# One graph-transformer layer on one core: keys and values of five blocks read during the last product job, the loads among the last messages spread anew, and two blocks of attention numerators instead of three ahead of the block loop

## The chip, the cores and the metric

The kernel runs on one core of one Trainium2 chip. The metric is the device time of that core in microseconds (us); lower is better. Of the runs of a kernel the median counts. A profile is one further execution, recorded instruction by instruction. Engines are called by their short names: PE (TensorE) multiplies matrices, with its weight loads as PEld; DVE (VectorE) and ACT (ScalarE) work element by element; POOL (GpSimd) here mainly issues gathers and loads; SP only issues DMAs.

## The reference

One layer on a graph with 1250 nodes, 1024 features and 20000 edges of 8 types. A relational graph convolution, a gate, a linear attention over all nodes and a feed-forward network with operands rounded to FP4 are added up, all in float32:

```python
xn = layernorm(x)
u  = xn @ root + bias + sum_r mean_{edges of type r into node}(xn[src]) @ weight[r]
z  = concat([u, xn]) @ w_gate + b_gate
h  = tanh(u) * z + xn * (1 - z)
# attention: 8 heads of 16; q and k are expanded to (1, a, a_i * a_j / sqrt(2))
kv, ks = sum_n k[n] v[n]^T, sum_n k[n]
mix = ((q @ kv) / max(q . ks, 1e-5)) @ w_out
x1 = x + h + mix
out = x1 + fp4(silu(fp4(ln(x1)) @ fp4(wg).T) * (fp4(ln(x1)) @ fp4(wu).T)) @ fp4(wd).T
```

## The kernel before, in words

The rows are 10 blocks of 128 nodes (`NB`, `BR`; the last has 98). The program is written as one list of steps for a tile framework, which puts waits between engines by itself. Each engine works its own list strictly in order. `issue_after(x)` adds an order: what is written inside stands after instruction x.

**Product jobs.** `product` (L532) multiplies all rows with one 1024 x 512 half of a weight matrix, as three matmuls of reduced-precision parts, called limbs (high, low and a difference; L552, L553, L554). `limb` cuts the next job's weights on DVE and ACT (L509 to L512) while the last piece of the present job runs. A job has nine pieces (blocks 0 and 1 together, then one block each). Counted from 0, jobs 0 to 12 are the relations (5 first halves, 8 second halves), 13 is QKV (written to `qkv_d`), 14 and 15 the root weight, 16 and 17 the lower half of the gate weight. Results go to DRAM (`y_d`, `root_d`, `gx_d`).

**Messages.** The 20000 sorted edges are 157 tiles (`ST`). For each feature half, a message gathers 128 rows of `y_d` (POOL, L464), scales them (ACT `hi` L475, DVE rest L477), builds a 0/1 matrix (DVE `sel` L473), sums rows of the same target with two matmuls (PE L480, L481), copies the sum (ACT L482) and stores it in `seg_d` (ACT's queue, L483). A gather is issued two tiles (`LAG`) before its use; there are 4 gather buffers and 2 to 3 of the others. Messages of half 0 go between the pieces of the jobs 5 to 12, those of half 1 between the pieces of 13 to 17, up to tile `EARLY` = 140. The rest comes after the last product.

**After the last product** (the `late` part, L726 on): one load of queries, keys and values of all blocks (L732, L733, on SP's queue); `mix_sums` (L735), the sums over all nodes; `mix_pairs(b)` (L750), products of keys and values on DVE (`kk`, L759) summed by PE (L763); `open_rows`, `open_first`, `open_rest`, which add up targets that cross tiles and end with a copy `osum` on ACT and an indirect add into `seg_d` (L831). A list `rest` of 13 of these has the remaining messages between its entries; from its entry 3 on each entry also issues one load of the list `behind` on POOL's queue (x, root and gx rows of blocks 0 and 1, `loads`, L660; four parts of the upper gate weight `wg`, L865) and, at first, one FFN weight load. Then follow `nodes` (the indirect gathers of summed messages into `u`, L666), the transposes of FFN weights (`ffn_weight`, L857), `mix_num(b)` for `FIRST` = 3 blocks (L670; the attention numerators: PE, then about 9 us of DVE), `mix_transposed`, and `gate_first` (L717), the first half of block 0's gate (L715). The load of `wo` comes last (L901).

**Block loop** (L981 to L996). `block(i)` adds u's parts (L925 or L929), transposes u, multiplies by `wg` (L937) and the attention by `wo` (L940), makes x1 (L944) and its FP4-rounded normalisation x2 (L948 on, quantiser lines L142 to L155). Then come `mix_num` of a block two ahead, `hidden` of the block before (transposes of x2, L163; L962) and `finish` of the one before that (L978).

Of the kernel before, what the change touches and what calls it, by code (L numbers as in the profile page):

```python
# [20 lines left out]
KC = D // 128  # L21
# [5 lines left out]
H, DH = 8, 16  # L27
FIRST = 3
LAG = 2
EARLY = 140  # L30
FW = 5
# [9 lines left out]
def block_rows(b):  # L41
    return slice(b * BR, min((b + 1) * BR, N))
# [7 lines left out]
def gps_layer(ctx: ExitStack, tc: tile.TileContext, x, src, dst, et, w_rel, w_root, bias,  # L50
# [466 lines left out]
    with ExitStack() as main:  # L517
# [106 lines left out]

        tiles = messages(1, 0, EARLY)
        for i in range(5):
            product(n0 + R + i, share(tiles, i, 5))
    limbs.close()
# [30 lines left out]

    def loads(b, q):  # L660
        loaded[b] = [ld.tile([BR, D], F32, name=name)[:rows_of(b)] for name in ("xt", "rt", "gx", "u")]
        return [lambda o=o, a=a: q.dma_start(o, a[block_rows(b), :])
                for o, a in zip(loaded[b], (x, root_d, gx_d))]
# [61 lines left out]
    with ExitStack() as late:  # L725
        op = late.enter_context(tc.tile_pool(name="op", bufs=1))  # L726
        pb = late.enter_context(tc.tile_pool(name="pb", bufs=4))
        fw = late.enter_context(tc.tile_pool(name="fw", bufs=FW))
        V.memset(kv[:, :, 256:257], 1.0)

        full, rest_n = (NB - 1) * BR, N - (NB - 1) * BR
        nc.sync.dma_start(qkv[:, :NB - 1, :384], qkv_d[:full, :].rearrange("(b p) c -> p b c", p=BR))  # L732
        nc.sync.dma_start(qkv[:rest_n, NB - 1, :384], qkv_d[full:, :])  # L733

        def mix_sums():  # L735
            ps = mm_tile()
            for b in range(NB):
                T.matmul(ps[:, :257], kv[:rows_of(b), b, :128], kv[:rows_of(b), b, :], start=(b == 0), stop=(b == NB - 1))
            V.scalar_tensor_tensor(h3(rl[:, :128]), h3(ps[:, :128]), 0.5, m8(DH), op0=ALU.mult, op1=ALU.mult)
            V.tensor_tensor(h3(rl[:, 128:256]), h3(ps[:, 128:256]), m8(DH), ALU.mult)  # L740
            V.tensor_scalar(rl[:, 256:264], mask8, ps[:, 256:257], None, op0=ALU.mult)
            ps = mm_tile()
            for b in range(NB):
                T.matmul(ps[:1, :128], ones[:rows_of(b), :1], kv[:rows_of(b), b, 128:256], start=(b == 0), stop=(b == NB - 1))
            V.tensor_copy(crow[:, :128], ps[:1, :128])
            V.memset(crow[:, 128:], float(N))

        bd_ps = []

        def mix_pairs(b):  # L750
            if b == 0:
                bd_ps.append(mm_tile())
            ps, n = bd_ps[0], rows_of(b)
            kks = []
            for c in range(4):
                kk = pb.tile([BR, 2, DH, DH], F32, name="kk")[:n]
                ck = kv[:n, b, c * 32:c * 32 + 32].rearrange("p (h i) -> p h i", h=2)
                cv = kv[:n, b, 128 + c * 32:128 + c * 32 + 32].rearrange("p (h e) -> p h e", h=2)
                V.tensor_tensor(kk, ck[:, :, None, :].to_broadcast([n, 2, DH, DH]),  # L759
                                cv[:, :, :, None].to_broadcast([n, 2, DH, DH]), ALU.mult)  # L760
                kks.append(kk.rearrange("p h e i -> p (h e i)"))
            for c, kk in enumerate(kks):
                T.matmul(ps[32 * c:32 * c + 32], kv[:n, b, 32 * c:32 * c + 32], kk,  # L763
                         start=(b == 0), stop=(b == NB - 1))
# [57 lines left out]


        s1, s2 = {}, [op.tile([128, HD], F32, name=f"s2{nh}") for nh in range(2)]
        for nh in range(2):
            V.memset(s2[nh][:B2], 0.0)

        def open_add(nh, i, n, ps):
            osum = op.tile([128, HD], F32, name="osum", bufs=2)
            evac(osum[:n], ps[:n])  # L830
            return G.indirect_dma_start(  # L831
                out=seg_d[nh][:, :], out_offset=bass.IndirectOffsetOnAxis(ap=orow[:n, i:i + 1], axis=0),
                in_=osum[:n, :], in_offset=None, compute_op=ALU.add).ins
# [20 lines left out]
        def ffn_weight(q, src, r0, n, c0, wide, o, chunks, col):  # L854
# [8 lines left out]

        behind = loads(0, G)
        behind += [lambda k=k: G.dma_start(wg[:, k:k + 2, :], w_gate[k * 128:(k + 2) * 128, :].rearrange(  # L865
            "(k p) n -> p k n", p=128)) for k in range(0, KC, 2)]
        behind += loads(1, G)
        there = []
        rest = [mix_sums, open_rows, lambda: (open_first(0), open_rest_rows(0), open_rest(0), open_first(1))]
        rest += [lambda b=b: mix_pairs(b) for b in range(NB)]  # L870
        done = EARLY
        for i, p in enumerate(rest):
            p()
            while done < ST + LAG and (done - EARLY) * len(rest) < (i + 1) * (ST + LAG - EARLY):
                message(1, done)
                done += 1
            if i >= 3:
                with tc.issue_after(gathered_last[0]):
                    behind.pop(0)()
                if len(there) < FW:  # L880
                    there.append(ffn_weight(S, *weights[len(there)]))

# [8 lines left out]
        with tc.issue_after(gathered_last[0]):  # L891
            for b in range(2):
                nodes(b, 0)
            open_rest_rows(1)
        for p in steps[:SUMS]:
            p()
        open_rest(1)
        gate_first()
        for p in steps[SUMS:]:
            p()  # L900
        nc.sync.dma_start(wo, w_out)  # L901
    first_nums = last_num[0]
# [3 lines left out]

    wk = ctx.enter_context(tc.tile_pool(name="wk", bufs=1))
    def block(b):

        rows, n = block_rows(b), rows_of(b)  # L910
        if b not in loaded:
            for p in loads(b, nc.sync):
                p()
        xt, rt, gx, u = loaded[b]
        with tc.issue_after(gathered_last[0]):
            for nh in range(0 if b >= 2 else 1, 2):
                nodes(b, nh)
# [9 lines left out]
        else:  # L927
            with tc.issue_after(first_nums):
                V.tensor_tensor(u, rt, u, ALU.add)  # L929
# [13 lines left out]
        x1 = wk.tile([BR, D], F32, name="x1", bufs=3)[:n]  # L943
        V.tensor_tensor(x1, sx, gx, ALU.add)  # L944

# [7 lines left out]

    def hidden(x1, x2):

        n = x1.shape[0]
        xqT = wk.tile([128, KC, BR], F32, name="xqT")
        transpose_cols(xqT, x2, n, D_CHUNKS, 0)
        pg, pu = mm_tile(), mm_tile()
# [23 lines left out]
    for i in range(NB + 2):  # L983
        if i < NB:
            ahead[i] = block(i)
        if i == 0:
            sums.close()
            psum_pools(ctx, "right", more=2)
        if i and i + FIRST - 1 < NB:
            mix_num(i + FIRST - 1)  # L990
        if i and i + FIRST - 2 < NB:
            mix_transposed(i + FIRST - 2)
        if 0 <= i - 1 < NB:
            hidden_rows[i - 1] = hidden(*ahead.pop(i - 1))
        if i >= 2:
            finish(i - 2, *hidden_rows.pop(i - 2))  # L996


# [25 lines left out]
```

## Time and profile before

| | us |
|---|---|
| runs | 1996.54, 1984.03, 1994.1 |
| median | 1994.1 |
| profiled execution | 1983.85 |
| its span, first to last instruction | 1982.1 |
| PE busy | 1869.1 (94%) |
| DVE, ACT, POOL busy | 1308.5, 747.7, 617.0 |
| mean granted TensorE clock | 0.974 |

The profiled execution is 10 us below the median, so a sum made from its rows is compared with 1983.85 first. Product jobs fill the time up to 1484.4 us; the stretch with the remaining messages lasts to 1577.5 us (last L481), then come the open sums and first gates, and block 1's gate starts at 1621.8 us. Busy times count an engine's instructions without its waits; a wait is listed with the engine and line that ended it. PEclk is the clock that the throttle granted, and the DMA share is the mean busy share of the 16 DMA engines.

### The profile page before, as it was taken

To read this page: it belongs to the slowest core of one execution; us is meant where nothing else is said; L and a number is where in the kernel's file an instruction comes from. 1 tells how busy PE (TensorE), PEld (TensorE's weight loads), DVE (VectorE), ACT (ScalarE), POOL (GpSimd) and SP (SyncE) were. 2 spreads that over 40 slices of the span, in tenths; PEclk is the share of its full clock that TensorE was granted. 3 is DMA by queue.
4 is the path that set the end of the run, shared out by engine and by line. 5 is a ranking of instruction groups with operands and counts; after the bars stand their busy time and mean duration, and the time that the engine had idled before them with its cause. 6 is when DMAs were issued, how large, how long until landed. Compare 5 with 4: busy or idle time off the path is not lost. (4 is left out here: it accounts for less than half of the span.)

```text
span 1982.1 us, 24076 instructions
## 1 busy us (share of the span) xinstructions
PE 1869.1 (94%) x7828; PEld 1272.4 (64%) x7828; DVE 1308.5 (66%) x2934; ACT 747.7 (38%) x1299; POOL 617.0 (31%) x590
## 2 busy tenths in 40 slices
PE   7999999999999999999999989999997888999998
PEld 5465447777777777777777877667673244544544
DVE  7988936777644566456546666766655758777765
ACT  5111421221224455545554455555553342222211
POOL 1022477885013233333332233343344410000000
PEclk9999999999999999999999999899897898999999
DMA  6266334444336767777676688777688842122100
GB/s 217 75 162 143 86 80 107 128 126 124 118 118 212 230 222 222 229 226 231 214 232 219 213 259 256 239 254 240 219 258 260 307 126 67 64 75 72 35 22 30
DMA packets 157976, 332.76 MB, mean 168 GB/s; under 512 B 26978, under 2 KB 34598, under 8 KB 157850
## 3 DMA queue, kind: packets, MB, share of 16 engines
q0 software_dynamic: 39616, 112.32, 21.9%
q10 hardware_dynamic: 77258, 142.48, 19.4%
q1 hardware_dynamic: 40976, 76.42, 12.4%
q8 instruction: 62, 1.02, 0.2%
q14 instruction: 64, 0.52, 0.1%
HBM read 184.41 MB, written 146.53 MB: 167 GB/s over the span
## 5 line engine op out<-in xcount | busy, mean ns | idle before, releaser
L552 PE MATMUL ab<-wH,xH 128*128 128x512 f32 (+2 forms) x1440 | 568.4, 395 | 3.1 <-issue 1.7
L554 PE MATMUL ab<-wD,xD 128*128 128x512 f32 (+2 forms) x1440 | 561.5, 394 | 5.1 <-DVE wD L512 4.6
L553 PE MATMUL ab<-wL,xL 128*128 128x512 f32 (+2 forms) x1440 | 564.8, 393 | 0.0
L464 POOL DMA_INDIRECT msg<-y_d,key x314 | 329.5, 1049 | 662.6 <-PE sm L481 333.6
L477 DVE SCALAR_TENSOR_TENSOR msg<-msg,weight,hi 128x512 fp32r<-128x512 f32 x314 | 234.0, 748 | 143.0 <-ACT hi L475 84.5
L554 PEld LDWEIGHTS ab<-wD,xD 128*128 128x128 f32 (+1 forms) x1440 | 268.1, 187 | 76.1 <-DVE wD L512 11.8
L552 PEld LDWEIGHTS ab<-wH,xH 128*128 128x128 f32 (+1 forms) x1440 | 270.3, 188 | 65.8 <-issue 2.7
L553 PEld LDWEIGHTS ab<-wL,xL 128*128 128x128 f32 (+1 forms) x1440 | 269.5, 187 | 63.9 <-DVE wL L511 0.5
L482 ACT COPY seg<-sm 128x512 f32<-128x512 f32 x314 | 182.4, 585 | 199.1 <-PE sm L481 150.8
L475 ACT ACTIVATE hi<-msg,weight 128x512 fp32r<-128x512 f32 x314 | 221.6, 721 | 80.2 <-DMA msg<-y_d,key 27.4
L390 POOL DMA_INDIRECT sort_d<-pay,row x160 | 208.3, 1302 | 61.6 <-issue 48.5
L560 ACT ACTIVATE yt<-ab 128x512 f32<-128x512 f32 (+2 forms) x180 | 106.1, 593 | 316.4 <-PE ab L553 276.1
L408 PE MATMUL mm<-wt,xnT 128*128 128x512 f32 (+1 forms) x480 | 220.9, 603 | 0.0
L561 DVE SCALAR_TENSOR_TENSOR yt<-ab,yt 128x512 f32<-128x512 f32 (+2 forms) x180 | 121.5, 680 | 146.5 <-ACT yt L560 140.4
L480 PE MATMUL sm<-hi,sel 128*128 128x512 f32 x314 | 133.9, 430 | 30.4 <-ACT hi L475 24.1
L481 PE MATMUL sm<-msg,sel 128*128 128x512 f32 x314 | 137.0, 436 | 24.4 <-DVE msg L477 24.4
L473 DVE TENSOR_SCALAR sel<-iota_n,last_row 128x128 fp32r<-128x128 f32 x314 | 89.6, 287 | 99.0 <-PE sm L481 94.7
L408 PEld LDWEIGHTS mm<-wt,xnT 128*128 128x128 f32 (+1 forms) x480 | 85.5, 188 | 86.6 <-issue 86.1
L510 ACT CAST wH<-h 128x512 fp32r<-128x512 f32 x144 | 88.6, 621 | 129.6 <-DVE h L509 117.2
L937 PE MATMUL mm<-wg,uT 128*128 128x512 f32 (+1 forms) x288 | 126.4, 592 | 0.0
L511 DVE TENSOR_TENSOR wL<-raw,h 128x512 fp32r<-128x512 f32 x144 | 98.1, 681 | 26.5 <-PE mm L408 26.5
L962 PE MATMUL mm<-wguT,xqT 128*128 128x352 f32 (+1 forms) x320 | 101.2, 476 | 10.7 <-ACT xqT L93 10.7
(281 smaller groups left out, 1981.6 us busy)
## 6 DMA issues: line engine op xcount, KB each, us to landing
seg_d<-seg ACTq DMA_DIRECT2D x314, 256.0 KB
y_d<-yt ACTq DMA_DIRECT2D x144, 256.0 KB
raw<-in_L_gnn_weight_dram SPq DMA_DIRECT2D x104, 256.0 KB
db<-in_dst_dram POOLq DMA_DIRECT2D x32, 305.2 KB
xt<-in_x_dram SPq DMA_DIRECT2D x16, 512.0 KB
wt<-in_L_gnn_weight_dram SPq DMA_DIRECT2D x24, 256.0 KB
msg<-y_d,key POOLq DMA_INDIRECT x314
lb<-lo_d POOLq DMA_DIRECT2D x32, 156.2 KB
```

The source lines that it names most:

```text
L390: st = G.indirect_dma_start(out=sort_d[:, :], out_offset=bass.IndirectOffsetOnAxis(ap=row[:, t:t + 1], axis=0), in_=pay[:, t, :], in_offse ...
L408: T.matmul(ps[:n], xnT[:, k, block_rows(b)], held[k], start=(k == 0), stop=(k == KC - 1))
L464: gathered_last[0] = G.indirect_dma_start(out=msg[:, :], out_offset=None, in_=y_d[nh][:, :], in_offset=bass.IndirectOffsetOnAxis(ap=key[:, ...
L475: S.mul(hi, msg, weight[:, t:t + 1])
L477: V.scalar_tensor_tensor(lo, msg, weight[:, t:t + 1], hi.bitcast(F32), op0=ALU.mult, op1=ALU.subtract)
L480: T.matmul(ps, sel, hi, start=True, stop=False)
L481: T.matmul(ps, sel, lo, start=False, stop=True)
L482: S.copy(seg, ps)
L552: T.matmul(pa[:p, :n], xH[:, k, ns], Wh[:, :n], start=(k == 0), stop=False)
L553: T.matmul(pa[:p, :n], xL[:, k, ns], Wl[:, :n], start=False, stop=(k == KC - 1))
L554: T.matmul(pb[:p, :n], xD[:, k, ns], Wd[:, :n], start=(k == 0), stop=(k == KC - 1))
L937: T.matmul(gates[nh][:n], uT[:, k, :n], wg[:, k, cs], start=(k == 0), stop=(k == KC - 1))
```

## The change

- Two blocks instead of three of `mix_num` ahead of the loop; the loop makes the third.
- `EARLY` goes from 140 to 135, and in the last job the messages are spread over seven pieces instead of nine.
- At the start of the last job, SP's queue loads keys and values of blocks 0 to 4 (128 KB each) into buffers of weights (`raw`, `h`) that no later job needs. The late load brings only blocks 5 to 9, and a third one the queries of 0 to 4. `mix_sums` is in two parts (blocks 0 to 4, 5 to 9) with `mix_pairs` of blocks 0 and 1 between; `open_rows` and the open sums follow. Messages of the late part stand after the latest summing matmul.
- Among the late messages POOL issues only root of block 0, two of four gate weights, x and gx of block 0, from entry 9 of `rest` on. The other two gate weights, block 1's rows and `wo` go to ACT's queue after the last `osum` copy.
- Before the loop only block 0's rows of `nodes(., 0)` are gathered; block 1 gathers both its halves itself.
- The sum of u in block b stands after x1 of block b-1, and no longer after the last `mix_num` ahead of the loop.
- In the loop the transposes of x2 stand ahead of `mix_num`, and `mix_transposed` at the end.

```diff
-FIRST = 3
+FIRST = 2
-EARLY = 140
+EARLY = 135
...
+        kv_early = []
         for i in range(5):
-            product(n0 + R + i, share(tiles, i, 5))
+            if i == 4:
+                for b in range(5):
+                    t = rawp.tile([128, HD], F32, name="raw") if b < 3 else topp.tile([128, HD], F32, name="h")
+                    V.memset(t[:, 256:257], 1.0)
+                    nc.sync.dma_start(t[:, :256], qkv_d[block_rows(b), 128:384])
+                    kv_early.append(t[:, :257])
+            product(n0 + R + i, share(tiles, i, 5), 0, 9 if i < 4 else 7)
...
-        nc.sync.dma_start(qkv[:, :NB - 1, :384], qkv_d[:full, :].rearrange("(b p) c -> p b c", p=BR))
+        nc.sync.dma_start(qkv[:, 5:NB - 1, :384], by_block(5 * BR, full, 384))
         nc.sync.dma_start(qkv[:rest_n, NB - 1, :384], qkv_d[full:, :])
+        nc.sync.dma_start(qn[:, :5, :], by_block(0, 5 * BR, 128))
...
-            evac(osum[:n], ps[:n])
+            evac(osum[:n], ps[:n]) if i == 0 else copied.append(S.copy(osum[:n], ps[:n]).ins)
...
-        behind = loads(0, G)
-        behind += [lambda k=k: G.dma_start(wg[:, k:k + 2, :], w_gate[k * 128:(k + 2) * 128, :].rearrange(
+        gate_w = [lambda q, k=k: q.dma_start(wg[:, k:k + 2, :], w_gate[k * 128:(k + 2) * 128, :].rearrange(
             "(k p) n -> p k n", p=128)) for k in range(0, KC, 2)]
-        behind += loads(1, G)
+        x_0, root_0, gx_0 = loads(0)
+        behind = [root_0, gate_w[0], gate_w[1], x_0, gx_0]
...
-        rest = [mix_sums, open_rows, lambda: (open_first(0), open_rest_rows(0), open_rest(0), open_first(1))]
-        rest += [lambda b=b: mix_pairs(b) for b in range(NB)]
+        rest = [lambda: mix_sums(0, 5)] + [lambda b=b: mix_pairs(b) for b in range(2)]
+        rest += [lambda: mix_sums(5, NB), open_rows,
+                 lambda: (open_first(0), open_rest_rows(0), open_rest(0), open_first(1))]
+        rest += [lambda b=b: mix_pairs(b) for b in range(2, NB)]
...
-                message(1, done)
+                with tc.issue_after(summed_kv[0]):
+                    message(1, done)
...
-            if i >= 3:
+            if i >= 3 and len(there) < FW:
+                there.append(ffn_weight(S, *weights[len(there)]))
+            if i >= 9:
                 with tc.issue_after(gathered_last[0]):
-                    behind.pop(0)()
-                if len(there) < FW:
-                    there.append(ffn_weight(S, *weights[len(there)]))
+                    behind.pop(0)(G)
...
         with tc.issue_after(gathered_last[0]):
-            for b in range(2):
-                nodes(b, 0)
+            nodes(0, 0)
             open_rest_rows(1)
...
         open_rest(1)
+        with tc.issue_after(copied[-1]):
+            for p in gate_w[2:] + loads(1):
+                p(S)
+            S.dma_start(wo, w_out)
         gate_first()
         for p in steps[SUMS:]:
             p()
-        nc.sync.dma_start(wo, w_out)
+        mix_transposed(FIRST - 1)
...
-            for nh in range(0 if b >= 2 else 1, 2):
+            for nh in range(0 if b else 1, 2):
...
-            with tc.issue_after(first_nums):
+            with tc.issue_after(summed[0]):
                 V.tensor_tensor(u, rt, u, ALU.add)
...
-        V.tensor_tensor(x1, sx, gx, ALU.add)
+        summed[0] = V.tensor_tensor(x1, sx, gx, ALU.add).ins
...
-        if i and i + FIRST - 1 < NB:
-            mix_num(i + FIRST - 1)
-        if i and i + FIRST - 2 < NB:
-            mix_transposed(i + FIRST - 2)
-        if 0 <= i - 1 < NB:
-            hidden_rows[i - 1] = hidden(*ahead.pop(i - 1))
+        if 1 <= i <= NB:
+            x1, x2 = ahead.pop(i - 1)
+            xqT = transposed(x2)
+        if 1 <= i < NB - 1:
+            mix_num(i + 1)
+        if 1 <= i <= NB:
+            hidden_rows[i - 1] = hidden(x1, xqT)
         if i >= 2:
             finish(i - 2, *hidden_rows.pop(i - 2))
+        if 1 <= i < NB - 1:
+            mix_transposed(i + 1)
```

`transposed(x2)` is the first half of the old `hidden`: it makes `xqT` with `transpose_cols`, as before.

More of the change, by code (lines that the diff above doesn't have):

```diff
@@ L658, in gps_layer, with loads @@
     nums, loaded, last_num = {}, {}, [None]
-    def loads(b, q):
+    def loads(b):
         loaded[b] = [ld.tile([BR, D], F32, name=name)[:rows_of(b)] for name in ("xt", "rt", "gx", "u")]
-        return [lambda o=o, a=a: q.dma_start(o, a[block_rows(b), :])
+        return [lambda q, o=o, a=a: q.dma_start(o, a[block_rows(b), :])
                 for o, a in zip(loaded[b], (x, root_d, gx_d))]
@@ L728, in gps_layer @@
         fw = late.enter_context(tc.tile_pool(name="fw", bufs=FW))
-        V.memset(kv[:, :, 256:257], 1.0)
+        V.memset(qkv[:, 5:, 384:385], 1.0)
         full, rest_n = (NB - 1) * BR, N - (NB - 1) * BR
-        nc.sync.dma_start(qkv[:, :NB - 1, :384], qkv_d[:full, :].rearrange("(b p) c -> p b c", p=BR))
+        by_block = lambda r0, r1, c: qkv_d[r0:r1, :c].rearrange("(b p) c -> p b c", p=BR)
+        nc.sync.dma_start(qkv[:, 5:NB - 1, :384], by_block(5 * BR, full, 384))
         nc.sync.dma_start(qkv[:rest_n, NB - 1, :384], qkv_d[full:, :])
[L735 to L746, printed above, removed]
@@ new lines, in gps_layer, with kv_of, mix_sums @@
+        nc.sync.dma_start(qn[:, :5, :], by_block(0, 5 * BR, 128))
+        sums_ps, summed_kv = [], [None]
+        def kv_of(b, c0, c1):
+            n = rows_of(b)
+            return kv_early[b][:n, c0:c1] if b < 5 else kv[:n, b, c0:c1]
+        def mix_sums(b0, b1):
+            if b0 == 0:
+                sums_ps.extend(mm_tile() for _ in range(2))
+            ps, pc = sums_ps
+            for b in range(b0, b1):
+                T.matmul(ps[:, :257], kv_of(b, 0, 128), kv_of(b, 0, 257), start=(b == 0), stop=(b == NB - 1))
+            for b in range(b0, b1):
+                summed_kv[0] = T.matmul(pc[:1, :128], ones[:rows_of(b), :1], kv_of(b, 128, 256),
+                                        start=(b == 0), stop=(b == NB - 1)).ins
+            if b1 == NB:
+                V.scalar_tensor_tensor(h3(rl[:, :128]), h3(ps[:, :128]), 0.5, m8(DH), op0=ALU.mult, op1=ALU.mult)
+                V.tensor_tensor(h3(rl[:, 128:256]), h3(ps[:, 128:256]), m8(DH), ALU.mult)
+                V.tensor_scalar(rl[:, 256:264], mask8, ps[:, 256:257], None, op0=ALU.mult)
+                V.tensor_copy(crow[:, :128], pc[:1, :128])
+                V.memset(crow[:, 128:], float(N))
@@ L756, in mix_pairs @@
                 kk = pb.tile([BR, 2, DH, DH], F32, name="kk")[:n]
-                ck = kv[:n, b, c * 32:c * 32 + 32].rearrange("p (h i) -> p h i", h=2)
-                cv = kv[:n, b, 128 + c * 32:128 + c * 32 + 32].rearrange("p (h e) -> p h e", h=2)
+                ck = kv_of(b, c * 32, c * 32 + 32).rearrange("p (h i) -> p h i", h=2)
+                cv = kv_of(b, 128 + c * 32, 128 + c * 32 + 32).rearrange("p (h e) -> p h e", h=2)
                 V.tensor_tensor(kk, ck[:, :, None, :].to_broadcast([n, 2, DH, DH]),
@@ L762, in mix_pairs @@
             for c, kk in enumerate(kks):
-                T.matmul(ps[32 * c:32 * c + 32], kv[:n, b, 32 * c:32 * c + 32], kk,
+                T.matmul(ps[32 * c:32 * c + 32], kv_of(b, 32 * c, 32 * c + 32), kk,
                          start=(b == 0), stop=(b == NB - 1))
@@ L821, in rows127 @@
             return seg_d[nh][:ZERO, :].rearrange("(t p) c -> t p c", p=128)[:, 127, :]
+        copied = []
         s1, s2 = {}, [op.tile([128, HD], F32, name=f"s2{nh}") for nh in range(2)]
@@ L907, in gps_layer @@
     wk = ctx.enter_context(tc.tile_pool(name="wk", bufs=1))
+    summed = [first_nums]
     def block(b):
@@ L911, in block @@
         if b not in loaded:
-            for p in loads(b, nc.sync):
-                p()
+            for p in loads(b):
+                p(nc.sync)
         xt, rt, gx, u = loaded[b]
         with tc.issue_after(gathered_last[0]):
-            for nh in range(0 if b >= 2 else 1, 2):
+            for nh in range(0 if b else 1, 2):
                 nodes(b, nh)
@@ L952, in block, with transposed, hidden @@
         return x1, x2
-    def hidden(x1, x2):
+    def transposed(x2):
+        xqT = wk.tile([128, KC, BR], F32, name="xqT")
+        transpose_cols(xqT, x2, x2.shape[0], D_CHUNKS, 0)
+        return xqT
+    def hidden(x1, xqT):
         n = x1.shape[0]
-        xqT = wk.tile([128, KC, BR], F32, name="xqT")
-        transpose_cols(xqT, x2, n, D_CHUNKS, 0)
         pg, pu = mm_tile(), mm_tile()
```

## The prediction

> **What bounds the kernel now.** I read the busy rows and the 40 slices first, then windows of 5 to 25 us where a slice dips, then the waits and the chain inside those windows.
>
> ```profile
> PE   7999999999999999999999989999997888999998
> PEclk9999999999999999999999999899897898999999
> DMA  6266334444336767777676688777688842122100
> ```
>
> PE (TensorE) is busy 1869.1 of 1982.1 us and sets the end nearly everywhere. Only where its row shows 7 or 8 (slices 31 to 34, 1486 to 1684 us) or its clock drops is there time that reordering can win; a slice is 49.6 us.
>
> Windows of 5 us at the end of product job 15 (columns: us, then busy us and instructions of PE, PEld, DVE, ACT, POOL, then PE clock, DMA share, GB/s):
>
> ```profile
> 1320.00:1325.00 5.00, 5.00 (x22) 3.41 (x21) 2.81 (x6) 2.74 (x6) 2.04 (x3) 1.00 0.81 257
> 1325.00:1330.00 5.00, 2.61 (x6) 1.06 (x5) 3.75 (x7) 2.63 (x5) 1.89 (x2) 0.86 0.81 255
> 1330.00:1335.00 5.00, 3.08 (x5) 1.29 (x5) 2.60 (x5) 2.92 (x5) 1.89 (x2) 0.50 0.77 240
> 1335.00:1340.00 5.00, 4.87 (x14) 3.42 (x13) 4.26 (x9) 3.43 (x7) 1.47 (x1) 0.62 0.89 277
> ```
>
> Inside a job PE does 22 to 23 matmuls in 5 us. Here 15 us held 6+5+14 = 25, which take 25/23 x 5 = 5.4 us elsewhere: 9.6 us lost. A clump of message matmuls (L480, L481) stands there with no product matmul between them; each pair waits up to 1.3 us for ACT's and DVE's halves (L475, L477). The ends of jobs 14 and 16 hold 30 and 24 in 15 us (8.5 and 9.8 us lost).
>
> The stretch after the last product (1484.4 us):
>
> ```profile
> 1490.00:1495.00 5.00, 2.31 (x3) 0.79 (x3) 1.64 (x12) 1.21 (x2) 1.59 (x2) 0.50 1.03 386
> 1495.00:1500.00 5.00, 0.00 (x0) 0.00 (x0) 0.51 (x1) 0.03 (x1) 0.00 (x0) 0.50 1.05 385
> 1500.00:1525.00 25.00, 22.96 (x82) 13.82 (x82) 17.42 (x50) 12.59 (x21) 11.52 (x9) 0.74 0.62 202
> 1525.00:1550.00 25.00, 19.71 (x56) 4.85 (x56) 14.85 (x27) 6.84 (x11) 17.52 (x17) 0.86 0.93 270
> 1550.00:1575.00 25.00, 19.80 (x59) 6.31 (x59) 17.57 (x32) 11.53 (x20) 10.62 (x13) 0.80 1.03 399
> 1575.00:1600.00 25.00, 21.28 (x79) 9.55 (x79) 13.33 (x27) 4.75 (x10) 4.69 (x4) 0.93 0.33 104
> 1600.00:1625.00 25.00, 21.03 (x93) 11.38 (x92) 18.16 (x35) 13.75 (x31) 0.74 (x1) 1.00 0.41 129
> ```
>
> PE stops wholly for one load, then works at a low clock while the DMA engines are full until 1575 us; after that they are a third full. The chain and the waits say who is late:
>
> ```profile
> 1485.82 13.64 DMA qkv<-qkv_d
> ...
> 1543.04 9.08 DMA msg<-y_d,key
> ...
> 1553.42 8.55 DMA seg_d<-seg
> ```
>
> ```profile
> DVE kk L759 <- DMA qkv<-qkv_d: 7.2, 1, 7.2
> PE sm L481 <- DVE msg L477: 8.8, 5, 7.1
> DVE u L929 <- issue: 4.4, 1, 4.4
> ```
>
> The keys' and values' load of 1.77 MB takes 13.64 us. DVE stands in front of it (kk, 7.2 us), the message's L477 stands behind kk, and PE behind that (7.1). Later a message gather takes 9.08 us and a segment store 8.55.
>
> **The change, part by part, against the profiled execution (1983.85 us: span 1982.1 and 1.75 around it).**
>
> *Ends of jobs.* In the changed program's instruction order the starts of jobs 15, 16 and 17 have product matmuls of the new job among the message pairs, with two or three pairs in a row instead of five; the start of job 14 keeps six. The DVE limb operations of such a boundary (8 x 3 x 0.62 = 15 us) still stand with L477 in one queue, so not all goes. I take 4 of about 9 us at three ends: **-12** (0 to -22).
>
> Here a rule speaks against the row. TensorE: Matmul & The Clock Gate (The HAM clock gate) has PE drop to half clock after an idle window of about 3.4 us. No wait here passes 1.3 us, so by the rule alone a thinner clump wins idle time only: 15 - (2.61+3.08+4.87) = 4.4 us per end, and 3 x 2 = 6 in all. The row shows 0.50 and 0.62 all the same, so half clock is there to win: 9.6 per end. My 4 lies between.
>
> *Two messages fewer beside products.* EARLY 140 to 135 makes it 29 instead of 27 after the last product matmul: 2 x 2 x 0.23 = **-0.9** there, and two more behind. That stretch took 92 us (1485.4 to the last L481 at 1577.5) for 27, and 14 of them were the stall: (92 - 14)/27 = 2.9 each, **+5.8** (1.7 if only PE's 2 x 2 x 0.43 count).
>
> *Keys and values early.* Five SP loads of 128 KB go out as the last job starts, when its last limb (DVE L511 at 1427.6) has freed their tiles, some 55 us before use. SP has no weights left to load there; products cover the transfers (0.65 MB at 255 GB/s is 2.6 us). The five memsets cost 0.07 us each on DVE. The late load shrinks to 0.94 MB plus 0.33 MB of queries. At the old 130 GB/s the first lands after 7.2 us, about 1493-95; its first reader now stands behind five blocks' sums, block 0's pairs and five messages, about 1499. So the 7.2 us wait of kk goes: **-7** (0 to -11, the idle PE of 1485-1500). The other sums are only split.
>
> *Loads among the messages.* Between 1527 and 1567 us POOL issued ten: 4 MB of gate weights and six of 512 KB. Now 3.5 MB of that (wg2, wg3, x1, root1, gx1) leave; the gate weights wg0, wg1 and root0 come late. At 399 GB/s 3.5 MB are 8.8 us of full DMA engines. A gather or store of 9 us was alone on the chain twice; PE still has its own work at low clock. I take **-5** (0 to -9). The rule against it is DMA: Bandwidth & Descriptors (Issuing engines are not separate DMA queues): all queues run on the same 16 engines, so another issuer saves only issue time. That would be nothing for PE (POOL's issues are 0.6 to 0.8 us each, beside its gathers). But the loads also move in time, from share 1.03 to share 0.33, and that row decides.
>
> *After the messages.* The last open sum's copy C was at 1584.5 and the first block's second gate half S at 1614.4: 29.9 us, in which mix_num(1) and (2) ran one after the other on DVE (the second from 1602.9 to 1612.0), and u's add L925 waited for the second (1611.91). With one fewer, up to 9 us go; but FFN down weights must still be transposed ahead of S, behind loads which now stand behind wo, and ACT first issues seven DMAs (0.33 to 0.6 each, about 3.5 us) ahead of its copies. **-5** (-8 to +20).
>
> *Start of the loop.* DVE stood 4.4 us (L929) for block 1's or 2's late half rows in front of block 0's normalisation; with the sum of block b held until x1 of b-1 this goes, but block 1's gate now waits for x1 of block 0 (PE idle about 5.6 us). Both stand on PE's path; block 0's x2 comes at about S+28 instead of S+32. Net **-1.2** (-2 to +5).
>
> *The loop.* A period with mix_num is 37.15 us (PE 35.3 of it, DVE 27.9), one without 33.0: the third mix_num costs **+4.1** here. The x transposes ahead of mix_num end the wait in this row (10.7 us in nine blocks):
>
> ```profile
> L962 PE MATMUL mm<-wguT,xqT 128*128 128x352 f32 (+1 forms) x320 | 101.2, 476 | 10.7 <-ACT xqT L93 10.7
> ```
>
> Of 1.2 to 1.6 us per block I expect 0.6 back in new waits on the two transpose banks: about 0.8 x 8 = **-6**. Both together -2 (-9 to +5).
>
> **Sum:** -12 -0.9 +5.8 -7 -5 -5 -1.2 -2 = -27.3, so 1956.5. The runs' median of 1994.1 is 1.0052 of the profiled 1983.85; so **1967**. Its own range, from the ends of its larger terms, is 1948 to 1985.
>
> **Rivals.**
> *A. Ends stay.* Messages are paced by gather, ACT and DVE; PE meets the same lag at each boundary. For it: DVE's 15 us of limbs. Against: other matmuls stand between. The -12 goes to -2, the loads' -5 to 0: -12, so 1972, median 1982: within 1%.
> *B. The burst after C, slower.* Seven transfers of 4.0 MB start together on ACT's queue. wo is last; PE's L940 (mm from wo) stands in order ahead of the down transposes and of S, and SP's down loads stand behind wo's lane. At 399 GB/s wo lands at C+10 to 14 and nothing waits (needed about C+17 to 22). At 104 GB/s (the 1575-1600 row, which shows what was asked for, not what could be had) it lands at C+40, loads and transposes add 11: S at C+51, 21 later than before, and half clock after. -27.3 +5 +21 + 4 (half clock) + 6 (block 1's late rows) = +9: 1993, median 2003. It decides from about 4 MB/20 us = 200 GB/s down. For it: the qkv load got 130 GB/s. Against: that was under full engines, and after C few gathers are left.
> *C. The loop pays.* Transposes ahead of mix_num make PE wait for x2 (DVE L155) each block, with mix_num behind it. With 4 us more in eight periods it is +32 +6: 1995, median 2005. Against: DVE is idle 9 us per period, and PE waited for L155 only once (4.1).
> *D. The load isn't the stall.* The edit does not do what it says, because messages were late anyway in 1485-1500, or the later half of the load is late in its place: -7 is 0, 1964, median 1974.
>
> **How the numbers follow.** Main case 0.50; A 0.22; B 0.13; C 0.05; D 0.10. Low 1945 is the main case with the ends at -22 and loads at -9; high 2007 takes in A, D and most of B and C. A measurement of this kernel can tell about 1%, 20 us, from no change: faster means below 1974. Of the main case 0.8, half of D and 0.2 of A lie there: 0.50. Above 2014 lie the worse halves of B and C and mishaps that I do not see: 0.15. The rest is 0.35.
>
> **What would show it.** Right: at the ends of jobs 14 to 16 no 5 us window with under 10 matmuls; no wait of kk on qkv, and PE busy over 3 of each 5 us from 1485; gathers under 6 us before the last message; from C to S 25 us; a period of 36 to 36.5 us. Wrong: clocks of 0.50 at the same ends; PE waiting for wo, or SP's down loads issued after it lands; transposes of x (L163) waiting for DVE's L155; a last message that ends as far after the last product as before (92 us).

## The result and the profile after

The changed kernel takes 2002.22 us (median of eight runs, 1997.7 to 2012.39); the kernel before took 1989.36 (eight runs). The ratio is 1.0068, with a 95% interval of 1.0042 to 1.0093: slower by 0.7%. The forecast was 1967, in a range of 1945 to 2007, and faster.

The profiled execution has a span of 1995.9 us, 13.8 more than before. Its slices of PE, of the granted clock and of the DMA engines:

```profile
PE   8999999999999999999999989989878889999998
PEclk9999999999999999999999989989988889999999
DMA  6265334444346776777767677777785651222100
```

The dips have moved but are as many as before. Between marks that exist in both traces the time went as follows (us; one profile each; L554 and L481 are counted at the start of their last matmul):

| stretch | before | after | difference | forecast |
|---|---|---|---|---|
| start to the first store of QKV results (not touched) | 1124.3 | 1118.5 | -5.8 | 0 |
| to the last product matmul | 361.1 | 362.8 | +1.7 | -12.9 |
| to the last message matmul (L481): the message stage | 92.2 | 103.9 | +11.7 | -6.2 |
| to the last osum copy (C) | 7.0 | 9.2 | +2.2 | 0 |
| to block 0's second gate half (S) | 29.9 | 30.0 | +0.1 | -5 |
| to block 0's first FFN matmul (L962, now L992) | 33.9 | 34.9 | +1.0 | -1.2 |
| to the end | 333.7 | 336.7 | +3.0 | -2 |

The first row, which the change does not touch, lies between 1118 and 1125 in all profiles here, so single stretches are not good to better than some 5 us.

At the end of job 15, the windows of after (same columns as before):

```profile
1320.00:1325.00 5.00, 3.00 (x12) 1.73 (x10) 3.33 (x7) 2.85 (x6) 3.38 (x3) 1.00 0.67 215
1325.00:1330.00 5.00, 4.11 (x8) 2.32 (x9) 3.70 (x8) 3.61 (x7) 2.14 (x3) 0.52 0.89 279
1330.00:1335.00 5.00, 5.00 (x19) 3.99 (x18) 4.67 (x10) 3.35 (x6) 1.05 (x1) 0.79 0.88 280
1335.00:1340.00 5.00, 2.33 (x9) 1.58 (x9) 1.81 (x4) 0.62 (x1) 0.00 (x0) 0.89 0.63 238
```

The hole of 25 matmuls in 15 us is gone, and there are two smaller ones: 48 matmuls in 20 us, where 22 to 23 in 5 us are the full rate. These are still 20 - 48/23 x 5 = 9.6 us lost. Counted in the same way, the ends of jobs 14 and 16 lose 1 and 3 us less than before, and the clock stays at 1.00 at the end of job 16. But over the five jobs PE stood idle for 26.6 us (336.2 of 362.8 busy) instead of 20.5 (340.6 of 361.1), so nothing of it is left in the sum. In the last window DVE, ACT and POOL are nearly idle too, so PE isn't waiting for messages there. The waits of the product jobs (1130 to 1482 us) tell for what; the first line had no time under PE before, the second had 2.8:

```profile
PE ab L554 <- DVE wD L512: 8.5, 5, 2.7
...
DVE h L509 <- DMA raw<-in_L_gnn_root_dram: 5.6, 3, 2.9
```

PE now comes to the new job's matmuls before their limbs are made, and the limbs in turn wait for the weights' loads: each of the four longest waits for wD comes about 1.1 us after a wait of DVE for `raw`.

The start of the message stage, which was to lose its stall:

```profile
1485.00:1490.00 5.00, 2.81 (x4) 1.15 (x4) 4.92 (x10) 2.51 (x5) 3.05 (x3) 0.57 1.03 355
1490.00:1495.00 5.00, 1.58 (x2) 0.57 (x2) 2.39 (x13) 1.46 (x3) 1.33 (x2) 0.50 1.06 400
1495.00:1500.00 5.00, 2.74 (x7) 2.21 (x8) 2.79 (x4) 2.42 (x4) 0.71 (x1) 0.50 0.94 340
1500.00:1525.00 25.00, 23.95 (x86) 9.43 (x84) 13.55 (x30) 9.28 (x16) 7.44 (x7) 0.95 0.55 170
1525.00:1550.00 25.00, 18.38 (x55) 6.54 (x54) 14.00 (x38) 8.70 (x15) 9.12 (x9) 0.81 0.50 156
1550.00:1575.00 25.00, 19.77 (x47) 4.94 (x46) 13.39 (x27) 8.36 (x14) 13.45 (x13) 0.85 0.76 225
```

No wait of kk on the load of queries, keys and values is left, as forecast. But the DMA engines are as full until 1500 us as they were: segment stores, gathers and other loads fill them without it. From 1500 to 1550 they are only half busy, and still the stage is longer. The chain shows what stands on the path instead:

```profile
1514.15 6.85 DMA msg<-y_d,key
...
1533.56 8.89 DMA seg_d<-osum,orow
...
1554.22 8.37 DMA msg<-y_d,key
...
1574.83 8.69 DMA msg<-y_d,key
...
1597.17 15.76 DMA wo<-in_L_mix_w_out_dram
```

Gathers of 7 to 9 us are still there, and `wo`, last of the six transfers behind the osum copy (2 MB of gate weights, three of 512 KB and `wo`), lands 18.6 us after it (1612.93 against 1594.31).

### The profile page after: what moved, and what is told of

The parts are those of the page before. It is cut to its first block, busy times and chain, and to the rows that moved or that the text cites. A ratio compares the mean times of both kernels' runs of the same rounds, so it can differ in the third digit from the quotient of the medians.

```text
span 1995.9 us, 24149 instructions
## 1 busy us (share of the span) xinstructions
PE 1883.3 (94%) x7828; PEld 1272.4 (64%) x7828; DVE 1301.4 (65%) x2938; ACT 755.8 (38%) x1302; POOL 619.2 (31%) x585
## 5 line engine op out<-in xcount | busy, mean ns | idle before, releaser
L554 PE MATMUL ab<-wD,xD 128*128 128x512 f32 (+2 forms) x1440 | 560.2, 394 | 10.4 <-DVE wD L512 10.0
L554 PEld LDWEIGHTS ab<-wD,xD 128*128 128x128 f32 (+1 forms) x1440 | 267.7, 187 | 82.3 <-DVE wD L512 18.6
L560 ACT ACTIVATE yt<-ab 128x512 f32<-128x512 f32 (+2 forms) x180 | 105.5, 590 | 326.1 <-PE ab L553 304.2
L561 DVE SCALAR_TENSOR_TENSOR yt<-ab,yt 128x512 f32<-128x512 f32 (+2 forms) x180 | 121.6, 680 | 150.9 <-ACT yt L560 149.7
L481 PE MATMUL sm<-msg,sel 128*128 128x512 f32 x314 | 133.2, 424 | 16.2 <-DVE msg L477 16.0
L674 POOL DMA_INDIRECT u<-seg_d,node_at x20 | 26.3, 1314 | 257.8 <-PE tr L681 199.1
```

The source lines that it names most:

```text
L481: T.matmul(ps, sel, lo, start=False, stop=True)
L554: T.matmul(pb[:p, :n], xD[:, k, ns], Wd[:, :n], start=(k == 0), stop=(k == KC - 1))
```

## The experiments

All are parts of the change, put onto the kernel before or taken out of the changed one. Each ratio is to the kernel before on the same chip, with its 95% interval; the kernels ran on several chips, so two of them are told apart by ratios whose intervals do not overlap, not by their medians. What the profiles showed, in us, is collected here: "products" from the first QKV store to the last product matmul, "left" the message matmul pairs that end after that (L481), "first sum" the start of the first summing matmul (L738, now L755) and "by 35" the L481 seen in the first 35 us, both from the last product matmul on; M is the message stage. Stages are from one profile each.

| kernel | ratio | products | left | first sum | by 35 | M | C to S | S to first FFN | from there to the end |
|---|---|---|---|---|---|---|---|---|---|
| before | 1 | 361.1 | 27 | 17.5 | 10 | 92.2 | 29.9 | 33.9 | 333.7 |
| changed | 1.0068 | 362.8 | 29 | 16.0 | 10 | 103.9 | 30.0 | 34.9 | 336.7 |
| u_early | 0.9990 | 370.0 | 27 | 12.5 | 13 | 87.5 | 29.8 | 35.2 | 337.4 |
| u_loads | 1.0062 | 361.7 | 29 | 18.1 | 10 | 108.5 | 24.4 | 35.2 | 337.4 |
| u_order | 1.0061 | 361.9 | 29 | 16.7 | 10 | 101.3 | 29.0 | 35.1 | 338.3 |
| k_alone | 0.9985 | 362.7 | 27 | 13.0 | 13 | 88.1 | 29.9 | 33.9 | 333.3 |
| a_alone | 1.0067 | 363.6 | 29 | 20.7 | 8 | 102.3 | 30.4 | 33.7 | 336.7 |
| u_early_7 | 1.0007 | 366.6 | 24 | 14.7 | 10 | 85.6 | 29.8 | 35.3 | 334.9 |
| k_sum | 0.9927 | 365.2 | 27 | 12.6 | 13 | 87.0 | 31.6 | 27.7 | 330.9 |
| k_ends | 1.0082 | 390.6 | 19 | 3.4 | 6 | 77.7 | 31.5 | 34.1 | 336.2 |
| k_sum_135 | 0.9947 | 359.2 | 31 | 6.2 | 13 | 92.6 | 30.0 | 27.7 | 332.7 |
| k_sum_tr | 0.9960 | 364.7 | 27 | 12.6 | 13 | 86.8 | 29.5 | 33.3 | 330.9 |
| k_sum_wg | 0.9939 | 365.7 | 27 | 13.0 | 13 | 86.5 | 38.0 | 27.8 | 331.5 |
| k_sum_135_7 | 0.9999 | 363.9 | 29 | 18.5 | 8 | 101.5 | 33.5 | 27.8 | 330.9 |

One reading fits all fourteen rows: the messages that are not through after 35 us ("left" less "by 35") take 3.2 to 3.9 us each for the rest of M. 14 of them remain in u_early, 19 in the changed kernel, 21 in a_alone.

**Taking parts out of the change.** u_early puts the sharing of messages back:

```diff
-EARLY = 135
+EARLY = 140
...
-            product(n0 + R + i, share(tiles, i, 5), 0, 9 if i < 4 else 7)
+            product(n0 + R + i, share(tiles, i, 5))
```

> Changed kernel with the share of messages beside the products put back (EARLY 140, nine pieces in the last job). Stages of the changed kernel: last product matmul 1481.2, from there to the last message matmul (L481) 104.0, from there to block 0's second gate half 39.2. Theory (the remaining messages are lengthened by the two more of them and by their order): products end back near 1485.5, message stage 104 to about 98, total 1 to 3 us below the changed kernel. Rival (job ends were won, nothing lost behind): 4 us above the changed kernel, the message stage stays 104.

Measured: 1991.47, ratio 0.9990 (0.9969 to 1.0012). The whole loss of 0.68% is gone, more than either side expected: M fell by 16.4 us, not by 6, of which the products took back 7.2 (370.0 against 362.8; no other kernel with nine pieces has them so long). So the sharing is what costs, and two messages fewer at 2.9 us each do not explain it.

u_loads puts the loads back among the messages, on POOL's queue, and wo on SP's:

```diff
-        behind = [root_0, gate_w[0], gate_w[1], x_0, gx_0]
+        behind = loads(0) + gate_w + loads(1)
...
-        with tc.issue_after(copied[-1]):
-            for p in gate_w[2:] + loads(1):
-                p(S)
-            S.dma_start(wo, w_out)
...
+        nc.sync.dma_start(wo, w_out)
```

> Changed kernel with the loads put back among the messages on POOL's queue and wo on SP's. Theory (behind the messages the burst on ACT's queue makes wo late and with it the down transposes): from the last message matmul to block 0's second gate half 39.2 falls to about 33; the message stage (104) grows by 0 to 5; total 2 to 6 us below the changed kernel. Rival (my prediction's step: full DMA engines were the pace of the messages): the message stage grows by 5 to 9 and the total is 3 to 8 us above the changed kernel.

Measured: 2001.68, ratio 1.0062 (1.0047 to 1.0077), no different from the changed kernel. The theory held in its stretches, though not in its total: M grew by 4.6 us, and from the last message to S it took 33.2 instead of 39.2 (from C on 24.4 instead of 30.0). The burst had won about what I forecast for the messages (5) and given it back at once (5.6). The 4.6 is not firm: u_order, below, has the changed kernel's order in this stage and differs from it by 2.6. This run moves the loads in time and from queue to queue together, so it does not test the rule on queues that I had set against this step.

u_order takes the `issue_after(summed_kv[0])` from around the late messages.

```diff
-                with tc.issue_after(summed_kv[0]):
-                    message(1, done)
+                message(1, done)
```

> Changed kernel without the rule that the late messages stand after the latest summing matmul. Theory (message matmuls held behind 20 sums and the first pairs leave the gathers without free buffers for 6 to 9 us, three times): the message stage falls from 104 to about 95, total 6 to 9 us below the changed kernel, about 1994. Rival (the gathers' transfers of 6 to 9 us set the pace whatever PE's order): message stage within 3 of 104, total within 3 of the changed kernel.

Measured: 2002.96, ratio 1.0061 (1.0046 to 1.0076). The order of PE's instructions in the stage came out the same without this rule, so this run does not test the theory it was meant for. It serves as a second measurement of the changed kernel: M 101.3 against 103.9, products 361.9 against 362.8.

**Parts alone on the kernel before.** k_alone has the early loads of keys and values and the smaller late load, with all sums ahead of open_rows and the pairs as before:

```diff
+            if i == 4:
+                for b in range(5):
+                    t = rawp.tile([128, HD], F32, name="raw") if b < 3 else topp.tile([128, HD], F32, name="h")
+                    V.memset(t[:, 256:257], 1.0)
+                    nc.sync.dma_start(t[:, :256], qkv_d[block_rows(b), 128:384])
+                    kv_early.append(t[:, :257])
...
-        rest = [mix_sums, open_rows, lambda: (open_first(0), open_rest_rows(0), open_rest(0), open_first(1))]
+        rest = [lambda: (mix_sums(0, 5), mix_sums(5, NB)), open_rows,
+                lambda: (open_first(0), open_rest_rows(0), open_rest(0), open_first(1))]
```

> The kernel before with one part of the change alone: keys and values of five blocks read at the start of the last job, the smaller late load, and the sums in two groups one after the other; everything else as before. My prediction's step: the wait of kk (7.2 us) goes and the total falls by 7, to 1982. Theory now (segment stores, gathers and the first loads fill the DMA engines until 1500 us anyway): DVE no longer waits for the late load, but the message stage (92.0 before) falls by 0 to 3 us only, total 1986 to 1990.

Measured: 1986.51, ratio 0.9985 (0.9968 to 1.0001): 3 us of the 7 by the ratio, with an interval that just takes in no gain; M 88.1 against 92.2. The late load was about half of the stall at most.

a_alone puts EARLY 135 and the seven pieces (the reverse of u_early's diff) on the kernel before. It also has the sums in two groups, as k_alone has them without a loss.

> The kernel before with the sharing of messages alone changed (EARLY 135, the last job's share over seven pieces), the loads and the loop as before. Theory: the sharing is what costs, by a longer message stage (92 before, 87.5 and 88.1 with early keys and values, 101 to 108 in three kernels with the new sharing): message stage 100 or more, job ends no better than 3 us, total 6 to 12 us above the kernel before. Rival: the new sharing costs only together with the new order of sums and pairs; alone it wins at the job ends, total 4 us below to 2 above the kernel before.

Measured: 2001.23, ratio 1.0067 (1.0041 to 1.0093). Alone the sharing costs as much as the whole change: M 102.3, and nothing won beside the products (363.6 against 361.1).

u_early_7 is the changed kernel with EARLY 140 and the seven pieces kept.

> Changed kernel with EARLY back at 140 but the last job's share still over seven pieces: 24 messages stay for the message stage instead of 29 (27 with nine pieces). In its order the stage begins as in the changed kernel: five messages close together, then ten sums with no message between. If the number of messages is what costs (2.9 us each), the stage is 75 to 80 us and the total 5 to 9 us below the one with nine pieces (1991.5). If the bunched order costs, the stage is 85 us or more and the total 1990 or more.

Measured: 1990.51, ratio 1.0007 (0.9992 to 1.0021), M 85.6. Three messages fewer than in u_early are left (24 against 27), and the stage is 1.9 us shorter, where 2.9 each would give 8.7. 10 messages were through after 35 us instead of 13, so 14 remained in both. The order took back what three messages fewer should have won; both numbers lie just inside the bounds that I had set for this.

**Job ends by themselves.** k_ends asks for all messages of the last five jobs in their first five pieces (k_alone with one line changed):

```diff
-            product(n0 + R + i, share(tiles, i, 5))
+            product(n0 + R + i, share(tiles, i, 5), 0, 5)
```

> Early keys and values alone on the kernel before, with the messages of each of the last five jobs asked for in its first five pieces of nine, so that no message matmul stands at a job's end or start: in the order the last piece has none and the first two at most one; 18 are left after the last product. If the clump at the boundary is what costs there (9 us at each of three ends), the products end 15 to 27 us earlier, and the message stage falls from 88 to about 65. If the limb chain (8 x 3 DVE operations behind the weight loads) bounds the boundary, the products end within 5 us of 1481, PE waiting for wD. If the messages' own pace bounds these jobs (2.5 to 2.8 us for each of 28), PE waits in the middle of the jobs instead, and the products end within 5 us of 1481 as well, without waits for wD.

Measured: 2002.55, ratio 1.0082 (1.0054 to 1.011). The products ended 28 us later than in k_alone (390.6 against 362.7). Windows in the middle and at the end of job 14:

```profile
1240.00:1245.00 5.00, 4.88 (x20) 3.63 (x21) 2.00 (x4) 3.14 (x5) 1.95 (x3) 1.00 0.85 284
1245.00:1250.00 5.00, 1.68 (x5) 0.67 (x4) 2.20 (x5) 3.01 (x6) 2.84 (x3) 0.98 0.86 244
...
1260.00:1265.00 5.00, 3.01 (x6) 1.06 (x6) 2.73 (x6) 2.89 (x6) 1.96 (x3) 0.84 0.70 202
1265.00:1270.00 5.00, 3.52 (x8) 2.40 (x9) 3.67 (x7) 3.87 (x7) 0.95 (x1) 0.50 0.84 281
1270.00:1275.00 5.00, 5.00 (x23) 3.71 (x22) 5.00 (x10) 1.81 (x4) 0.00 (x0) 0.98 0.57 182
1275.00:1280.00 5.00, 5.00 (x23) 4.05 (x22) 5.00 (x11) 1.66 (x3) 0.00 (x0) 1.00 0.60 184
```

From 1270 us the limb chain runs with DVE wholly busy, and PE does 23 matmuls in 5 us beside it. This boundary, without messages, costs nothing. The holes are now where seven pairs in a piece were asked for, and PE's waits from 1130 to 1480 us say the same:

```profile
PE sm L481 <- DVE msg L477: 13.1, 20, 0.8
PE sm L480 <- ACT hi L475: 11.1, 13, 1.9
PE ab L552 <- ACT yt L560: 7.9, 6, 1.8
```

There is no wait for wD among them, nor up to the last product at 1515.3 us. The third expectation held in kind, and its size was worse than expected (8 pairs more stand beside these products, but their 16 matmuls are only some 4 us): PE meets pairs whose halves ACT and DVE have not made yet, wherever they stand too close. With 28 messages in a job of about 79 us (1195.5 to 1354.5 us for two in the kernel before), one every 2.8 us is what each job has to take in. Neither of the two placements tried (k_ends and the change) gained anything; an even spread of single pairs was not tried.

**How many, or in which order?** k_sum_135 sets EARLY to 135 in k_sum (below), with nine pieces in every job.

> The kernel with early keys and values and the sums of u freed from block 2 on (k_sum, 1972.4), with EARLY 135 instead of 140 and nine pieces in each job: 31 messages stay after the last product instead of 27, with single messages between the first and last sums as before (7 there, against 8). If each message left over costs what the tails of the message stages show (3.2 to 3.75 us), the stage grows from 87 to about 101, and the total by 10 to 13, to 1982-1986. If only bunches cost, the stage stays below 92 and the total within 4 of 1972.

Measured: 1976.13, ratio 0.9947 (0.993 to 0.9965). M grew by 5.6 us for four messages, 1.4 each, well below my 3.5, and the products were 6.0 shorter. Leaving 31 messages to the end costs 4 us in the medians, and the intervals of the two ratios overlap. (In the traces 3 messages stand between the first and last sums of k_sum and 4 in k_sum_135, fewer than the 8 and 7 that I had expected.) k_sum_135_7 then changes one line:

```diff
-            product(n0 + R + i, share(tiles, i, 5))
+            product(n0 + R + i, share(tiles, i, 5), 0, 9 if i < 4 else 7)
```

> One line apart from k_sum_135 (1976.1; message stage 92.6 with 31 messages left): the last job's messages over seven pieces instead of nine. In its order 29 messages are left, but all twenty summing matmuls stand in one row with no message between them, where k_sum_135 had seven messages there. Theory (a row of sums without messages leaves the gathers' four buffers full and idle, and what is not done in the first 35 us costs over 3 us each behind): 7 to 10 messages done in the first 35 us instead of 13, message stage 98 or more, total 1982 to 1990 in spite of two messages fewer. Rival (the number left is what counts): message stage 86 to 92, total 1970 to 1976.

Measured: 1987.93, ratio 0.9999 (0.9979 to 1.002), M 101.5, with 8 messages through after 35 us. This is the expectation of the order, within all its bounds: two messages fewer, and slower by 0.5% by the ratios, 12 us by the medians. The first 20 us after the last product, k_sum_135_7 first (at 1484.2) and then k_sum_135 (at 1477.4):

```profile
1484.20:1494.20 10.00, 3.96 (x9) 1.50 (x7) 9.78 (x34) 4.85 (x9) 5.51 (x6) 0.80 0.91 300
1494.20:1504.20 10.00, 3.06 (x6) 1.82 (x7) 3.39 (x7) 3.61 (x6) 0.94 (x1) 0.50 0.91 348
```

```profile
1477.40:1487.40 10.00, 5.74 (x13) 2.99 (x12) 8.25 (x31) 4.29 (x7) 5.82 (x5) 0.77 0.97 337
1487.40:1497.40 10.00, 10.00 (x49) 6.64 (x47) 5.37 (x13) 4.81 (x8) 4.38 (x4) 0.89 1.00 356
```

The DMA engines are as full in the faster kernel, so their load alone doesn't make the difference. The two timelines at the first sum, in the same order:

```profile
1501.30 0.60 ACT L560 ACTIVATE yt<-ab 98x512 f32<-98x512 f32 x1 [3.02 <-DMA gx_d<-yt]
1501.93 0.69 DVE L561 SCALAR_TENSOR_TENSOR yt<-ab,yt 98x512 f32<-98x512 f32 x1 [3.95 <-ACT yt L560]
...
1502.72 1.62 PE L755 MATMUL mm<-raw 128*128 128x257 f32 x3 [5.06 <-issue]
```

```profile
1480.88 0.58 ACT L560 ACTIVATE yt<-ab 98x512 f32<-98x512 f32 x1
1482.73 0.67 DVE L561 SCALAR_TENSOR_TENSOR yt<-ab,yt 98x512 f32<-98x512 f32 x1
...
1483.51 1.20 PE L755 MATMUL mm<-raw 128*128 128x257 f32 x2
```

L560 and L561 copy the last product's sums out of PSUM (`ab`). The first summing matmul starts 0.1 us behind the end of the last L561 in 13 of the 14 profiles (0.5 in a_alone): its PSUM tile is cut from the banks that `ab` held. In six of them PE stands idle directly before it (0.9 to 5.1 us; 5.06 here), among them the changed kernel (2.8), u_loads and u_order. In the other eight, the kernel before among them, PE is at a message up to then. With the pairs bunched at the end of the job, three such copies were still to do when PE had finished (one in k_sum_135); the third waited for a store of `gx_d` to free one of two `yt` buffers, at a DMA share of 0.91. So the sums started 18.5 us after the last product instead of 6.2, stood in one row of twenty with no message between (9.4 us), and the gathers, which need one of four buffers back from PE, stopped from 13.8 to 28.8 us.

**The loop and its start.** k_sum is k_alone with the sums of u freed from block 2 on:

```diff
-            with tc.issue_after(first_nums):
+            with tc.issue_after(first_nums if b < 2 else summed[0]):
                 V.tensor_tensor(u, rt, u, ALU.add)
```

> Early keys and values alone on the kernel before, and the sums of u freed from block 2 on only: block 1's stays where it was. Reason: in the kernel before DVE waits 4.4 us for block 2's late half rows in front of block 0's normalisation; in the changed kernel that wait went (26.6 to 20.9 from block 1's gate to block 0's first FFN matmul), but block 1's gate came 6.7 us later (7.3 to 14.0). With block 1's kept: 7.3 and about 21, total 5 to 6 us below early keys and values alone (1986.5). Rival: DVE has as much to do before block 0's normalisation either way, total within 2 us of it.

Measured: 1972.38, ratio 0.9927 (0.989 to 0.9965). That is 14 us below k_alone (five runs here), where I had expected 5 to 6. From S to block 0's first FFN matmul it takes 27.7 us instead of 33.9: the wait of 4.4 us on DVE is gone, and block 1's gate starts 7.3 us after S as before, where it was 14.0 in the changed kernel. These 6.2 us are the expected gain, and stood alike in every later kernel with this line and the old loop order (27.7 to 27.8); the rest of the 14 isn't explained by the profiles.

k_sum_tr adds the loop order of the change to k_sum (x2's transposes first, mix_transposed last, still three mix_num ahead of the loop).

> k_sum (1972.4) with the loop order of the change: x2's transposes ahead of mix_num, mix_transposed last, still three mix_num ahead of the loop. My prediction's step: 6 us less (0.8 in each of eight blocks), 1966. Theory now (in the changed kernel the loop took 3 to 4 us more for its one mix_num of 4.1 more, so the order itself won 0 to 1): total within 2 us of k_sum.

Measured: 1979.79, ratio 0.9960 (0.9944 to 0.9976), slower than k_sum by 7 us in the medians, more than either side said, though the intervals of the two ratios overlap. What the profiles show is the stretch from S to the first FFN matmul, 33.3 us against 27.7. The chain into block 0's FFN in k_sum_tr, and in k_sum:

```profile
1635.37 1.95 PE tr L163 x8
...
1638.15 2.09 PE mm L688 x8
1640.24 1.18 PE mm L695 x2
1641.42 0.75 PE mm L696 x2
```

```profile
1638.41 0.67 PE tr L163 x4
...
1639.11 0.59 ACT xqT L93
...
1639.74 2.34 PE mm L986 x7
```

In k_sum mix_num (L688 to L696) ran while PE waited for x2. In the new order x2's transposes stand ahead of it, so it comes on the path, between the transposes and the FFN matmuls (from the end of the transposes to the FFN 4.9 us, against 0.7 here). In the later blocks the order does win: from one Silu to the next 36.4 to 36.8 us instead of 37.2. From the first FFN matmul on the sum is nil (330.9 both).

k_sum_wg is k_sum with two of the four gate weight loads taken from POOL's list:

```diff
-        behind = loads(0) + gate_w + loads(1)
+        behind = loads(0) + gate_w[:2] + loads(1)
...
+        with tc.issue_after(copied[-1]):
+            for p in gate_w[2:]:
+                p(S)
```

> k_sum (1972.4) with the last two gate weight loads (2 MB) taken from among the messages and issued on ACT's queue after the last osum copy; wo and all else as in k_sum. Theory: the 3.5 MB moved in the changed kernel shortened its message stage by 4.6 us (103.9 against 108.5), and what that won was lost to wo's late landing; here wo is early and three mix_num fill the time, so the stage falls by 2 to 4 us and the total with it: 1968 to 1970. Rival: block 0's second gate half waits for the weights (they land over 10 us after the copy) or ACT's issues delay the transposes: total 1972 or more.

Measured: 1974.93, ratio 0.9939 (0.9919 to 0.9959). M did not move (86.5 against 87.0), and C to S grew by 6.4 us. The total is the rival's, but its cause is not what the chain shows: the chain into S now goes over a row load of 2.98 us and ACT's sx behind it. And in the better order of messages, fewer bytes among them won nothing.

k_sum has the lowest median, 0.7% below the kernel before and 1.5% below the changed one (1972.38 against 2002.22); its interval overlaps those of k_sum_135, k_sum_tr and k_sum_wg.

## Why the prediction was wrong

**The sharing of messages: the step that failed.** I took "two messages fewer beside products" as -0.9 and +5.8, and the ends of jobs as -12: a gain of 7.1 in all. The products won nothing (361.1 to 362.8), and the stage lost 11.7. a_alone shows that this part costs 0.67%, about 13 us and the change's whole loss. Rival A had the ends right and took the stage as unharmed. The error had two halves. At the job ends I counted the hole as something that better places would fill; k_ends shows a boundary that is free without messages, and that the same holes open wherever pairs stand closer than ACT and DVE make them. The changed kernel split the hole at job 15, and added a new wait for limbs behind it, 8.5 us in all: the clump had been their cover. In the message stage I priced a message by the average (2.9 us) and did not look at how the changed order began. There twenty sums and their PSUM tile stand, and it matters how many messages get through in the first 35 us: 13 in every kernel of the nine-piece kind with early keys, 8 to 10 with seven pieces. (It was 10 in the kernel before too, which had two messages fewer left and waited for its keys.) What remained then took 3.2 to 3.9 us each, not 2.9.

**Keys and values early (-7).** The wait of kk on the load went, as forecast, but only 3 us came of it (k_alone). I had read the chain's "DMA qkv 13.64" as the cause; the same DMA engines stay full until 1500 us with stores and gathers, and the first sum still came 13.0 us after the last product in k_alone, against 17.5. Rival D had the right side of this, half way.

**Loads among the messages (-5) and after (-5).** The first came out in size (u_loads: 4.6, with the scatter said there). The second failed on wo: it landed 18.6 us behind C, inside the 17 to 22 that I gave as the need, and the chain to S goes from it over L967, the down transposes and a row load of 3.38 us, so that S stayed where it had been; without the burst C to S is 24.4. So the mechanism of rival B was there at about a quarter of its price (5.6 of 21). Its seven transfers are six. Their 4.0 MB in 18.6 us are 215 GB/s, just above the 200 where I had it decide, though the engines moved 288 GB/s in that time: the burst did not have them alone.

**Start of the loop (-1.2) and loop (-2).** Measured +1.0 and +3.0. Freeing the sum from block 2 on is worth 6.2 us (k_sum), but the changed kernel does not have it: there block 1's gate comes later (14.0 instead of 7.3 from S), and mix_num stands ahead of the FFN in the same stretch. What each of the two takes back was not split. I had set the gain against block 1's later gate, and had not seen that it can be had without it. In the loop the wait of L962 for xqT fell as forecast (10.7 to 0.6), and others took 6.9 us of it (hT 3.7, xqT at L681 2.1 and at L163 1.1): 0.6 us a block, not 0.8. What I had not priced is the first block, where mix_num lost its cover: 5.6 us in k_sum_tr.

**The clock.** I set 4 us per end between the Trainium skill's rule on idle windows of about 3.4 us (TensorE: Matmul & The Clock Gate, The HAM clock gate) and the row. The runs don't settle what an end is worth, since the holes did not close; but the row's side of it stands: in k_ends the clock fell to 0.50 where no single wait of PE in these jobs was above 1.9 us. I had read the rule's idle window as one unbroken wait of PE; here the clock fell without one.

## What to carry to other kernels

When a change moves work in a list that in-order engines share, read the first 20 us after the seam in the new order on each engine: which copy frees the next stage's PSUM, what it stands behind, and what has no buffer until then. A hole in PE's row is a symptom; ask what rate the producer behind it has, and how close together the new places ask for its work, before counting the hole as won. Work that fills a wait on the path (here mix_num, the clump of messages) is worth its cover: before moving it, say what will stand in the gap.

## What the runs showed of the hardware that I had not expected

A load of 512 KB (`wo` in the changed kernel) took 15.76 us as the last of 4.0 MB issued within 3.3 us; the DMA engines were full (share 1.03 to 1.04, 384 to 410 GB/s) for the first 10 us of it and at 0.60 for the rest. And the granted clock went to 0.50 in stretches where PE kept working with short waits only (1265 to 1270 us in k_ends: 3.52 of 5 us busy).

## What stays open

That the seven pieces together with EARLY 135 cost the time is shown by a pair of kernels that differ in one line, and by a_alone and u_early. Why they do is in part read from traces. That the late copy of the last product out of PSUM causes the late sums rests on six traces in which PE stands idle before them; a kernel in which that copy alone is earlier, say by a third `yt` buffer, was not tried. The messages ahead of the sums are late as well: in k_sum_135_7 the chain goes over a segment store of 8.05 us (L483) that ACT waits for. How much of the 12 us between that pair is the late start and how much the row of sums without messages is not split.
